# Two graph attention layers over 16 batches: layer 0's scores and V products in runs of two steps, tile additions in odd steps behind the minima, mask pieces later

## The chip, the cores and the metric

One core of one Trainium2 chip runs the whole program. The metric is device time in microseconds (us). Engines are named as in the profile: PE (TensorE, matmuls), PEld (its weight loads), DVE (VectorE), ACT (ScalarE), POOL (GpSimd), SP (SyncE, which issues most DMAs). SBUF is the on-chip memory of 128 partitions; PSUM is the memory that matmuls write.

## What is computed

The input x is 16 batches of 1024 rows by 256 features, adj is 16 matrices of 1024 by 1024 zeros and ones. Both layers are residual attention layers behind a layer norm and a ReLU:

```python
h = jnp.maximum(_layernorm(x), 0.0)
x = x + attention0(h, adj)        # 4 heads of 64, no biases but bo
h = jnp.maximum(_layernorm(x), 0.0)
x = x + attention1(h, adj)        # 8 heads of 32, bq, bk, bv, bo
# attention(h): q, k, v = h @ Wq, h @ Wk, h @ Wv, in heads
#   s = q k^T / sqrt(D);  s = where(adj > 0, s, -inf)
#   concat(softmax(s) v over heads) @ Wo + bo
```

All arithmetic is in float32; only the mask is held in 8 bits. Softmax is computed without subtracting a maximum; the sums are tested at the end (a slow program would run if a test failed; it did not run).

## The kernel before

**Steps.** The scores are held transposed, keys on the partitions. A *step* makes four blocks of 128 keys by 512 queries. Layer 0 has 16 steps per batch: two halves of the queries (`qh`), two groups of two heads (`g`), four steps `j` of two key tiles. Layer 1 has 32: `qh`, `g` (four heads), eight `j`. A step has these parts: `scores` (L364) makes four blocks in two PSUM pairs; `exponentials` takes for each pair VectorE's minimum with the mask (L380), which frees the pair, and ScalarE's exponential (L385); two steps later (`LEAD`) `weigh` (L396) multiplies by V into the group's PSUM tile `po`. PSUM score pairs come from one pool of three (`ps_s`), which K, Q, V, turns and output products (`pq`, `pv`, `ph`, `py`) use too.

**Row sums.** In layer 1 GpSimd adds the tiles of two steps (L482) and matmuls with ones count them (`count`, L273). In layer 0 `add_tiles` (L399 to L410) adds a step's two halves into a tile `t`: for `j` = 0 on GpSimd, for the others on VectorE (L407), and then GpSimd adds the tile of the step before (L409). The tiles come from a pool of three buffers. The last one of the group is counted once. Then `copy_out` (L280) copies the group's `po`, `spread` (L288 to L292) sends the sums through DRAM onto all partitions, `invert` (L297) takes reciprocals and sends them back by DRAM, `normalize` (L316) multiplies, `test` (L305 to L311) checks; `end_half` (L345, L350) makes the output product and adds it to x.

**Masks.** A mask comes in eight tiles: `load` (a DMA on POOL's queue, L121), `flip` (a transposing DMA on SP, L125), `put` (ScalarE, L131). The mask of layer 0 is then changed in place into that of layer 1 in eight pieces by VectorE (`second`, L139).

**Inputs of a section.** For each layer, batch and half: `stats` (VectorE, L160, L161), `norm` (ScalarE, L177), `add_bias` (GpSimd, L185), `turn` (transposes, L195), `k` and `q` (L207; copies L214, L220), `values` (L236).

**Order.** The order of everything is written out by hand; the engines run their queues in order of emission. All steps form one list: layer 0 of batch 0; then for each batch b layer 0 of b+1 and layer 1 of b. The table of due times (L597 to L641) says at which step each input, mask piece or load is emitted; `a` is the first step of layer 0 of b+1, and `c` that of layer 1 of b. `end_group` (L491 to L508) adds entries for the end of a group. `Stream.run` (L436 to L468) emits for each step i:

```python
if now: scores(now)
if i % 2 or not self.large(i):
    for st in waiting: weigh(st)          # else kept for the next step
    ...
exponentials(now, copy)                   # copy: between the two halves
add_tiles(step before), if layer 0
everything that is due at i
```

A *large* job (k, q, values, end_half) that is due at an even step puts off that step's weigh, so two steps' scores, then the large job, then two steps' scores and two weighs follow (a run of two). Where nothing large is due, scores and weigh alternate step by step.

**Start.** Before the stream (L511 to L567) come the loads of the first inputs, all eight flips and puts of mask 0, k, q and values of batch 0, and one product of `bv` with the output matrix (`pb`, L561), added to `bo` in `bo1` (L566).

Of the kernel before, what the change touches and what calls it, by code (L numbers as in the profile page):

```python
# [18 lines left out]
P = 128  # L19
EPS = 1e-5  # L20
HEADS = (4, 8)

LEAD = 2


SUM_MIN, SUM_MAX = 1e-15, 1e15
# [13 lines left out]
def load_weights(nc, const, a):  # L40

    w, loads = Weights(), []

    def mat(src, name):
        t = const.tile([P, 2, 256], F32, tag=name, name=name)
        loads.append((t, src.rearrange("(c p) f -> p c f", p=P)))
        return t

    def row(src, name):
        t = const.tile([P, 256], F32, tag=name, name=name)  # L50
        loads.append((t, src.partition_broadcast(P)))
        return t

    def col(src, name):
        t = const.tile([P, 2], F32, tag=name, name=name)
        loads.append((t, src.rearrange("(c p) -> p c", p=P)))
        return t

    w.k, w.q, w.v, w.o = [], [], [], []
    for layer in range(2):  # L60
        for kind, mats in (("k", w.k), ("q", w.q), ("v", w.v), ("o", w.o)):
            mats.append(mat(a[f"w{kind}{layer}"], f"w{kind}{layer}"))
    w.bo = [row(a["bo0"], "bo0"), row(a["bo1"], "bo1")]
    w.bq = col(a["bq1"], "bq1")
    w.bk = col(a["bk1"], "bk1")
    w.bv = col(a["bv1"], "bv1")
    w.ident = const.tile([P, P], F32, tag="ident", name="ident")
    make_identity(nc, w.ident)
    w.ones = const.tile([P, 64], F32, tag="ones", name="ones")
    nc.gpsimd.memset(w.ones, 1.0)  # L70
    w.mhalf = const.tile([P, 4], F32, tag="mhalf", name="mhalf")
    nc.gpsimd.memset(w.mhalf, -0.5)
    return w, loads


def fast_program(ctx, tc, a, w, loads, chk):
# [23 lines left out]

    def psum_pair(name):
        return ps_s.tile([P, 2, 512], F32, tag="ps_s", name=name)

    bo = [w.bo[0]]

    xs = {}

# [36 lines left out]
    class Inputs:  # L144
# [37 lines left out]
        def add_bias(self, half):  # L182

            rows = xs[self.b, half]
            nc.gpsimd.tensor_add(  # L185
                rows, rows, bo[self.layer].unsqueeze(1).to_broadcast([P, 4, E])
            )

        def turn(self, half):
# [56 lines left out]
    class Group:  # L246
# [21 lines left out]
        def count(self, p, start, stop):  # L268

            if start:  # L270
                self.s = ps_o.tile([P, 512], F32, tag="pz", name=f"pz_{self.n}")
            for r in range(self.per):
                nc.tensor.matmul(  # L273
                    self.s[r * self.D : (r + 1) * self.D, :], w.ones[:, : self.D], p[:, r, :],
                    start=start, stop=stop,
                )

        def copy_out(self):
            self.ob = work.tile([P, 512], F32, tag="o", name=f"o_{self.n}")
# [91 lines left out]
    def exponentials(st, between):  # L371
# [5 lines left out]
        for i in range(2):  # L377
# [6 lines left out]
            )  # L384
            nc.scalar.activation(half, half, AF.Exp, scale=gr.scale)  # L385
            if i == 0:
                between()

    def weigh(st):
        gr = st.gr  # L390
# [29 lines left out]
    class Stream:  # L420

        def __init__(self, steps):
            self.steps, self.due = steps, {}

        def large(self, i):
            return any(
                f.__name__ in ("k", "q", "values", "end_half") for f, _ in self.due.get(i, [])  # L430
            )

        def later(self, i, f, *args):
            self.due.setdefault(i, []).append((f, args))

        def run(self):  # L436
            steps = self.steps
# [2 lines left out]
            for i in range(n + LEAD):  # L440
# [2 lines left out]
                    waiting.append(steps[i - LEAD])  # L443
                if now:
                    scores(now)
                copy = lambda: None
                if i % 2 or not self.large(i):
                    for st in waiting:
                        weigh(st)
                    for st in waiting:  # L450
                        if st.gr.layer:
                            self.count_steps(i, st)
                        if st.last:
                            copy = st.gr.copy_out
                            self.end_group(i, st.gr)
                    waiting = []
                if now:
                    exponentials(now, copy)
                else:
                    copy()  # L460
                one = steps[i - 1] if 1 <= i <= n else None
                if one and one.gr.layer == 0:
                    add_tiles(one)
                for f, args in self.due.pop(i, []):
                    f(*args)
            while self.due:
                for f, args in self.due.pop(min(self.due)):
                    f(*args)  # L468
# [21 lines left out]

        def end_group(self, i, gr):  # L491

            if gr.layer == 0:
                i += 1
                self.later(i, gr.count, gr.t, True, True)
            elif not gr.hurry:
                i += 2
            self.later(i, gr.spread)
            if gr.hurry:
                self.later(i, gr.finish)  # L500
                self.later(i, gr.test)
                return
            self.later(i + 2, gr.invert)
            self.later(i + 3, gr.test)

            self.later(i + (5 if gr.layer and not gr.last else 4), gr.normalize)
            if gr.g == 1:
                self.later(i + (7 if gr.layer else 6), gr.end_half)  # L508

    def open_w(n):  # L510
        for _ in range(n):  # L511
# [13 lines left out]
    inp.stats(1)  # L525
    inp.turn(0)

    def tiles(*ts):
        for t in ts:
            mask.flip(t)  # L530
            (mask if t + 2 < NT else masks[1]).load((t + 2) % NT)
            open_w(-(-len(loads) // 2))

    tiles(0, 1)
    inp.k(0)
    inp.norm(1)
    inp.q(0)
    inp.turn(1)
    mask.put(0)
    mask.put(1)  # L540
    inp.values(0)
    tiles(2, 3)
    inp.k(1)
    mask.put(2)
    mask.put(3)
    tiles(4, 5)
    inp.q(1)
    mask.put(4)
    mask.put(5)
    tiles(6, 7)  # L550
    inp.values(1)
    mask.put(6)
    mask.put(7)
    for half in range(QH):
        open_x(1, half)
        inp.add_bias(half)


    pb = psum_pair("pb")[:, 0, :E]
    for c in range(2):  # L560
        nc.tensor.matmul(  # L561
            pb, w.bv[:, c : c + 1].to_broadcast([P, P]), w.o[1][:, c, :],
            start=(c == 0), stop=(c == 1),
        )
    bo1 = small.tile([P, E], F32, tag="bo1", bufs=1, name="bo1v")
    nc.vector.tensor_add(bo1, pb, w.bo[1])  # L566
    bo.append(bo1)  # L567

# [11 lines left out]
    stream = Stream(steps)  # L580
    later = stream.later

    def norms(inp, half, i):

        later(i, inp.stats, half, (0, 1))
        later(i + 1, inp.stats, half, (2, 3))
        later(i + 3, inp.norm, half, (0, 1))
        later(i + 4, inp.norm, half, (2, 3))
        later(i + 5, inp.add_bias, half)

    def half_inputs(inp, half, *at):

# [1 line left out]
            later(i, f, half)  # L594


    for t in range(NT):  # L597
        later(2 * t, masks[1].flip, t)
        later(2 * t + 1, masks[1].put, t)
        if t + 2 < NT:  # L600
            later(2 * t + 1, masks[1].load, t + 2)
    for half in range(QH):
        norms(inputs[0][1], half, 3 * half)
    half_inputs(inputs[0][1], 0, 5, 6, 8, 10)
    half_inputs(inputs[0][1], 1, 11, 12, 14, 16)
    for b in range(B - 1):
        mine, a, c = inputs[1][b], first[b + 1], second[b]
        if b == 0:

            norms(mine, 0, a + 1)  # L610
            norms(mine, 1, a + 9)
            half_inputs(mine, 0, a + 6, a + 8, a + 10, a + 12)
            half_inputs(mine, 1, a + 15, c, c + 4, c + 2)
        else:
            norms(mine, 0, a - 10)
            norms(mine, 1, a - 8)
            half_inputs(mine, 0, a - 4, a + 2, a + 4, a + 6)
            half_inputs(mine, 1, a - 2, a + 8, c + 4, c + 2)
        for kt in range(NT):
            later(a + 4 + kt, masks[b].second, kt)  # L620
        if b + 2 < B:
            other, mask = inputs[0][b + 2], masks[b + 2]
            later(a + 1, open_x, b + 2, 0)
            later(a + 11, open_x, b + 2, 1)
            norms(other, 0, a + 7)
            norms(other, 1, a + 15)
            half_inputs(other, 0, a + 14, c + 6, c + 10, c + 12)
            half_inputs(other, 1, c + 14, c + 16, c + 18, c + 20)
            for t in range(NT):
                i = a + 2 + 5 * t  # L630
                later(i, mask.load, t)
                later(i + 3, mask.flip, t)
                later(i + 5, mask.put, t)
        else:
            last = inputs[1][b + 1]
            norms(last, 0, c + 1)
            norms(last, 1, c + 9)
            half_inputs(last, 0, c + 6, c + 10, c + 12, c + 14)
            half_inputs(last, 1, c + 16, c + 20, c + 36, c + 34)
            for kt in range(NT):  # L640
                later(c + 8 + 2 * kt, masks[b + 1].second, kt)  # L641
    stream.run()
# [15 lines left out]

def careful_program(ctx, tc, a, w):

    nc = tc.nc
    x, adj, out = a["x"], a["adj"], a["out"]
    B, N, E = x.shape
    NT = N // P
    actp = ctx.enter_context(tc.tile_pool(name="cact", bufs=1))
    bv = actp.tile([P, E], F32, tag="bv", name="c_bv")
    nc.sync.dma_start(bv, a["bv1"].partition_broadcast(P))
# [6 lines left out]
    def layer_of(b, layer, xt):  # L674
# [26 lines left out]
        for t in range(NT):  # L701
            pv = ps_t.tile([P, E], F32, tag="t", name=f"c_pv_{layer}_{t}")
            for c in range(2):
                nc.tensor.matmul(
                    pv, hT[:, c, ts(t, P)], w.v[layer][:, c, :], start=(c == 0), stop=(c == 1)
                )
            if layer == 0:
                nc.scalar.copy(v[:, t, :], pv)
            else:
                nc.vector.tensor_add(v[:, t, :], pv, bv)  # L710
# [185 lines left out]
```

## Time and profile before

| what | us |
|---|---|
| median of 3 runs | 3406.17 (3405.55 to 3406.78) |
| the profiled execution | 3402.26 |
| its span | 3400.5 |
| busy: PE, DVE, POOL, ACT | 3359.3, 2468.8, 2446.0, 2188.1 |
| one period (layer 0 of one batch, layer 1 of the one before) | 209.40 |
| minimum L380, exponential L385, mean of one | 1.215, 1.057 |
| VectorE addition L407, median and mean | 1.219, 1.525 |
| GpSimd addition L409, mean; L482, mean | 2.495, 4.562 |
| mask piece L139, median and longest | 0.686, 4.417 |

The profile takes one execution. Its page lists for each engine the busy share, and for each line of the code the instructions: `p<-mask,ps 128x1024` reads as a tile p written from mask and ps, 128 partitions by 1024 elements, then the count, the busy time with the mean of one in ns, and the engine's idle time just before with what ended it (`<-PE ps L364` is a wait for the matmuls of that line). A timeline has start, duration, engine and line; it may join successive like instructions of one tile group in a row (x2, x8). A table by stretches has for each engine the busy time and, in brackets, the instructions; after them the granted clock of PE. Matmuls are float32, each with several passes, so that a block has more matmul rows than calls in the code.

### The profile page before, as it was taken

The numbers are of one execution on the slowest core, as the hardware profiler recorded it, in microseconds if no ns is written. First come the engines' busy times: TensorE is split into PE (matmuls) and PEld (weight loads), VectorE is DVE, ScalarE is ACT, GpSimd is POOL, SyncE is SP. The second block draws the span as 40 slices with busy tenths as digits, with TensorE's granted clock in tenths as the row PEclk, the third lists the DMA queues.
The fourth block names the chain that finished last, engine by engine and source line by source line (L and its number), as shares of the span: only waits on it lengthen the run. The fifth ranks groups of instructions, "written<-read, shape, count | busy, mean of one in ns | idle before, by whom it ended". The sixth has DMA issues, their size and how long they took to land. (4 is left out here: it accounts for less than half of the span.)

```text
span 3400.5 us, 46245 instructions
## 1 busy us (share of the span) xinstructions
PE 3359.3 (99%) x18190; PEld 1302.6 (38%) x18190; DVE 2468.8 (73%) x2664; ACT 2188.1 (64%) x2402; POOL 2446.0 (72%) x1606
## 2 busy tenths in 40 slices
PE   7999999999999999999999999999999999999998
PEld 3443343433434333343333334334343343433432
DVE  4676767777677776777767777677776777767876
ACT  5566666676666756667566675666756667565665
POOL 4577777777777776777668686686867768677777
PEclk9999999999999999999999999999999999999999
DMA  6212121211212122121111212112122111210001
GB/s 133 44 36 36 47 42 36 49 37 47 40 36 51 34 49 36 36 51 42 42 35 39 48 42 45 34 43 45 39 48 39 42 41 41 47 35 23 14 17 31
DMA packets 250737, 141.76 MB, mean 42 GB/s; under 512 B 182416, under 2 KB 217488, under 8 KB 250512
## 3 DMA queue, kind: packets, MB, share of 16 engines
q1 hardware_dynamic: 232080, 105.18, 12.6%
q0 software_dynamic: 18432, 33.56, 6.4%
q8 instruction: 144, 2.36, 0.3%
q14 instruction: 81, 0.66, 0.1%
HBM read 120.33 MB, written 18.34 MB: 41 GB/s over the span
## 5 line engine op out<-in xcount | busy, mean ns | idle before, releaser
L380 DVE SCALAR_TENSOR_TENSOR p<-mask,ps 128x1024 f32<-128x1024 fp8e4 x1536 | 1801.3, 1215 | 753.7 <-PE ps L364 729.1
L385 ACT ACTIVATE p<-p 128x1024 f32<-128x1024 f32 x1536 | 1618.2, 1057 | 984.1 <-DVE p L380 940.9
L482 POOL TENSOR_TENSOR p<-p,p 128x2048 f32<-128x2048 f32 x255 | 1163.0, 4562 | 399.9 <-PE po L396 396.1
L364 PE MATMUL ps<-qT,kT 32*128 32x512 f32 (+1 forms) x6144 | 1167.4, 633 | 13.1 <-DVE p L380 8.7
L396 PE MATMUL po<-p,v 128*32 128x512 f32 (+1 forms) x6144 | 989.9, 601 | 0.5 <-ACT o L280 0.5
L409 POOL TENSOR_TENSOR t<-t,t 128x1024 f32<-128x1024 f32 x192 | 479.1, 2495 | 401.3 <-DVE t L407 324.4
L364 PEld LDWEIGHTS ps<-qT,kT 32*128 32x128 f32 (+1 forms) x6144 | 375.0, 184 | 726.2 <-issue 364.0
L396 PEld LDWEIGHTS po<-p,v 128*32 128x32 f32 (+1 forms) x6144 | 229.1, 118 | 688.3 <-issue 529.3
L407 DVE TENSOR_TENSOR t<-p 128x1024 f32<-128x1024 f32 x192 | 292.7, 1525 | 0.9
L273 PE MATMUL pz<-p,ones 128*32 128x512 f32 x2056 | 267.8, 593 | 0.2 <-POOL p L482 0.2
L207 PE MATMUL pq<-hT,wk 128*128 128x512 f32 x512 | 240.0, 612 | 2.7 <-ACT hT L196 2.6
L236 PE MATMUL pv<-wv,hT 128*128 128x256 f32 x1024 | 237.9, 385 | 0.0
L345 PE MATMUL py<-wo,cat 128*128 128x256 f32 x1008 | 234.2, 385 | 2.5 <-DVE p L380 2.5
L207 PE MATMUL pq<-hT,wq 128*128 128x512 f32 x512 | 236.6, 605 | 0.0
L236 PEld LDWEIGHTS pv<-wv,hT 128*128 128x128 f32 x1024 | 189.4, 190 | 70.7 <-issue 36.1
L345 PEld LDWEIGHTS py<-wo,cat 128*128 128x128 f32 x1008 | 186.4, 190 | 73.2 <-issue 32.3
L316 POOL TENSOR_TENSOR cat<-o,inv 128x512 f32<-128x512 f32 x127 | 164.3, 1294 | 20.7 <-DMA inv<-vd 14.7
L407 POOL TENSOR_TENSOR t<-p 128x1024 f32<-128x1024 f32 x64 | 171.5, 2680 | 0.4
L131 ACT ACTIVATE mask<-adjT,mhalf 128x1024 fp8e4<-128x1024 bf16 x128 | 145.5, 1138 | 10.1 <-DMA adjT<-adj 10.1
L207 PEld LDWEIGHTS pq<-hT,wk 128*128 128x128 f32 x512 | 93.3, 192 | 144.3 <-issue 137.1
L207 PEld LDWEIGHTS pq<-hT,wq 128*128 128x128 f32 x512 | 92.1, 189 | 139.8 <-issue 128.5
L177 ACT ACTIVATE hn<-x,shift,rstd 128x256 f32<-128x256 f32 x256 | 138.1, 588 | 6.9 <-POOL shift L170 6.9
(52 smaller groups left out, 1567.8 us busy)
## 6 DMA issues: line engine op xcount, KB each, us to landing
adj<-in_adj_dram POOLq DMA_DIRECT2D x128, 256.0 KB, 3.6
x<-in_x_dram SPq DMA_DIRECT2D x32, 512.0 KB
inv<-vd SPq DMA_DIRECT2D x128, 128.0 KB
inv<-vd SPq DMA_DIRECT2D x252, 64.0 KB
out_dram<-x SPq DMA_DIRECT2D x31, 512.0 KB
adjT<-adj SPq DMA_TRANSPOSE x128
sd<-s SPq DMA_DIRECT2D x64, 4.0 KB
sn<-sd SPq DMA_DIRECT2D x64, 4.0 KB
```

The costliest lines, as they stand in the source:

```text
L207: nc.tensor.matmul(pq[:, m, :], wt[self.layer][:, c, ts(m, P)], self.hT[half][:, c, :], start=(c == 0), stop=(c == 1),)
L236: nc.tensor.matmul(pv[:, i, :], self.hT[half][:, c, ts(i, P)], w.v[self.layer][:, c, :], start=(c == 0), stop=(c == 1),)
L273: nc.tensor.matmul(self.s[r * self.D : (r + 1) * self.D, :], w.ones[:, : self.D], p[:, r, :], start=start, stop=stop,)
L316: nc.gpsimd.tensor_mul(self.half.cat[:, self.g, :], self.ob, self.inv)
L345: nc.tensor.matmul(py[:, i, :], self.half.cat[:, c, ts(i, P)], w.o[self.layer][:, c, :], start=(c == 0), stop=(c == 1),)
L364: nc.tensor.matmul(st.ps[i // 2][:, i % 2, :], gr.inp.kT[r * D : (r + 1) * D, gr.g, ts(kt, P)], gr.inp.qT[r * D : (r + 1) * D, gr.g, ts(gr ...
L380: nc.vector.scalar_tensor_tensor(out=half, in0=gr.mask.m[:, kt, ts(gr.qh, 512)].unsqueeze(1).to_broadcast([P, 2, 512]), scalar=BIG, in1=st ...
L385: nc.scalar.activation(half, half, AF.Exp, scale=gr.scale)
L396: nc.tensor.matmul(gr.o[r * D : (r + 1) * D, :], gr.inp.v[:, kt, h * D : (h + 1) * D], st.p[:, i, :], start=(kt == 0), stop=(kt == NT - 1),)
L407: engine.tensor_add(t, st.p[:, 0:2, :], st.p[:, 2:4, :])
L409: nc.gpsimd.tensor_add(t, t, gr.t)
L482: nc.gpsimd.tensor_add(one, one, st.p)
```

## The change

In `Stream.run`, a step of layer 0 with an even number never weighs: both steps' weighs come in the odd step. The tile additions of the two steps before are emitted in odd steps only, behind that step's minima. Counts are emitted ahead of the exponentials; layer 0's copy of `po` comes behind both. What is due at a step is sorted: small jobs first, turns and large jobs last. In `end_group` the delays change. In the start only masks 0's tiles 0 to 3 are flipped and put; tiles 4 to 7 and those of batch 1 follow at steps of the stream; the x of batch 1 is loaded earlier; layer 1's weights are loaded last; the product of `bv` moves to step 9. The due table is rewritten: layer 0's large jobs at odd steps, one k moved into layer 1's section, the pieces of `second` from a+5 on, two of them at a+7 and at a+11 each. The slow program's V bias is dropped; it does not run.

```diff
+LARGE = ("k", "q", "values", "end_half")
+COUNTS = ("count", "count_added")
...
+        def count_added(self):
+            self.count(self.t, True, True)
...
+        def rank(self, entry):
+            return entry[0].__name__ in ("turn", *LARGE)
...
-                copy = lambda: None
-                if i % 2 or not self.large(i):
+                copies = []
+                if i % 2 or not (now and now.gr.layer == 0 or self.large(i)):
                     for st in waiting:
                         weigh(st)
...
+                due = self.due.pop(i, [])
+                for f, args in due:
+                    if f.__name__ in COUNTS:
+                        f(*args)
                 if now:
-                    exponentials(now, copy)
+                    exponentials(now, copies if now.gr.layer else [])
+                    if now.gr.layer == 0:
+                        for f in copies:
+                            f()
...
-                one = steps[i - 1] if 1 <= i <= n else None
-                if one and one.gr.layer == 0:
-                    add_tiles(one)
-                for f, args in self.due.pop(i, []):
-                    f(*args)
+                if i % 2:
+                    for one in steps[max(i - 2, 0) : min(i, n)]:
+                        if one.gr.layer == 0:
+                            add_tiles(one)
+                for f, args in sorted(due, key=self.rank):
+                    if f.__name__ not in COUNTS:
+                        f(*args)
...
             if gr.layer == 0:
-                i += 1
-                self.later(i, gr.count, gr.t, True, True)
-            elif not gr.hurry:
-                i += 2
-            self.later(i, gr.spread)
...
-            self.later(i + 2, gr.invert)
-            self.later(i + 3, gr.test)
-            self.later(i + (5 if gr.layer and not gr.last else 4), gr.normalize)
+                self.later(i + 2, gr.count_added)
+                at = 2, 3, 4, 7
+            else:
+                at = (2, 3, 4, 8) if gr.last else (2, 4, 7, 9)
+            for k, f in zip(at, (gr.spread, gr.invert, gr.normalize)):
+                self.later(i + k, f)
+            self.later(i + at[1] + 1, gr.test)
             if gr.g == 1:
-                self.later(i + (7 if gr.layer else 6), gr.end_half)
+                self.later(i + at[3], gr.end_half)
...
-    mask.put(6)
-    mask.put(7)
...
+    def flip(u):
+        masks[u // NT].flip(u % NT)
+        if u + 2 < 2 * NT:
+            masks[(u + 2) // NT].load((u + 2) % NT)
+    def put(u):
+        masks[u // NT].put(u % NT)
...
+    flip(2)
+    open_x(1, 0)
+    flip(3)
+    open_w(5)
+    open_x(1, 1)
...
+    for u in range(4, 2 * NT):
+        later(u - 3, flip, u)
+        later(u - 2, put, u)
+    later(9, bias_of_v)
...
-            norms(mine, 0, a - 10)
-            norms(mine, 1, a - 8)
-            half_inputs(mine, 0, a - 4, a + 2, a + 4, a + 6)
-            half_inputs(mine, 1, a - 2, a + 8, c + 4, c + 2)
+            norms(mine, 0, a - 10, a - 9, a - 7, a - 6)
+            half_inputs(mine, 0, a + 1, a + 3, a + 5, a + 7)
+            norms(mine, 1, a - 8, a - 7, a - 5, a - 4)
+            half_inputs(mine, 1, a + 11, c + 2, c + 6, c + 4)
         for kt in range(NT):
-            later(a + 4 + kt, masks[b].second, kt)
+            later(a + 5 + (0, 2, 2, 4, 6, 6, 8, 10)[kt], masks[b].second, kt)
...
-            norms(other, 0, a + 7)
-            norms(other, 1, a + 15)
-            half_inputs(other, 0, a + 14, c + 6, c + 10, c + 12)
-            half_inputs(other, 1, c + 14, c + 16, c + 18, c + 20)
+            norms(other, 0, a + 5, a + 7, a + 9, a + 11)
+            half_inputs(other, 0, a + 13, c + 10, c + 12, c + 14)
+            norms(other, 1, c + 5, c + 7, c + 9, c + 10)
+            half_inputs(other, 1, c + 15, c + 18, c + 20, c + 24)
```

The new function `bias_of_v` holds the product that stood in the start, and writes `bo` in place instead of a tile of its own. `norms` and `half_inputs` take their steps one by one (turn, k, q, values); the entries of the first two and the last batches are shifted likewise.

More of the change, by code (lines that the diff above doesn't have):

```diff
@@ L59, in load_weights, with mats @@
     w.k, w.q, w.v, w.o = [], [], [], []
-    for layer in range(2):
-        for kind, mats in (("k", w.k), ("q", w.q), ("v", w.v), ("o", w.o)):
-            mats.append(mat(a[f"w{kind}{layer}"], f"w{kind}{layer}"))
+    def mats(layer):
+        for kind, of in (("k", w.k), ("q", w.q), ("v", w.v), ("o", w.o)):
+            of.append(mat(a[f"w{kind}{layer}"], f"w{kind}{layer}"))
+    mats(0)
     w.bo = [row(a["bo0"], "bo0"), row(a["bo1"], "bo1")]
@@ L66, in load_weights @@
     w.bv = col(a["bv1"], "bv1")
+    mats(1)
     w.ident = const.tile([P, P], F32, tag="ident", name="ident")
@@ L102, in psum_pair @@
         return ps_s.tile([P, 2, 512], F32, tag="ps_s", name=name)
-    bo = [w.bo[0]]
     xs = {}
@@ L185, in add_bias @@
             nc.gpsimd.tensor_add(
-                rows, rows, bo[self.layer].unsqueeze(1).to_broadcast([P, 4, E])
+                rows, rows, w.bo[self.layer].unsqueeze(1).to_broadcast([P, 4, E])
             )
@@ L386, in exponentials @@
             if i == 0:
-                between()
+                for f in between:
+                    f()
     def weigh(st):
@@ L429, in large @@
             return any(
-                f.__name__ in ("k", "q", "values", "end_half") for f, _ in self.due.get(i, [])
+                f.__name__ in LARGE for f, _ in self.due.get(i, [])
             )
@@ L453, in run @@
                         if st.last:
-                            copy = st.gr.copy_out
+                            copies.append(st.gr.copy_out)
                             self.end_group(i, st.gr)
                     waiting = []
+                due = self.due.pop(i, [])
+                for f, args in due:
+                    if f.__name__ in COUNTS:
+                        f(*args)
                 if now:
-                    exponentials(now, copy)
-                else:
-                    copy()
-                one = steps[i - 1] if 1 <= i <= n else None
-                if one and one.gr.layer == 0:
-                    add_tiles(one)
-                for f, args in self.due.pop(i, []):
-                    f(*args)
+                    exponentials(now, copies if now.gr.layer else [])
+                    if now.gr.layer == 0:
+                        for f in copies:
+                            f()
+                else:
+                    for f in copies:
+                        f()
+                if i % 2:
[5 more added lines that the diff above has]
+                        f(*args)
             while self.due:
@@ L491, in end_group @@
         def end_group(self, i, gr):
+            if gr.hurry:
+                for f in (gr.spread, gr.finish, gr.test):
+                    self.later(i, f)
+                return
             if gr.layer == 0:
-                i += 1
-                self.later(i, gr.count, gr.t, True, True)
-            elif not gr.hurry:
-                i += 2
-            self.later(i, gr.spread)
[L499 to L502, printed above, removed]
-            self.later(i + 2, gr.invert)
-            self.later(i + 3, gr.test)
-            self.later(i + (5 if gr.layer and not gr.last else 4), gr.normalize)
+                self.later(i + 2, gr.count_added)
[5 more added lines that the diff above has]
+            self.later(i + at[1] + 1, gr.test)
             if gr.g == 1:
-                self.later(i + (7 if gr.layer else 6), gr.end_half)
+                self.later(i + at[3], gr.end_half)
     def open_w(n):
@@ L526, in fast_program @@
     inp.turn(0)
[L528 to L534, printed above, removed]
+    def flip(u):
[4 more added lines that the diff above has]
+        masks[u // NT].put(u % NT)
+    flip(0)
+    flip(1)
+    open_w(1)
     inp.k(0)
@@ L538, in fast_program, with bias_of_v @@
     inp.turn(1)
-    mask.put(0)
-    mask.put(1)
+    put(0)
+    put(1)
     inp.values(0)
-    tiles(2, 3)
+    flip(2)
[3 more added lines that the diff above has]
+    open_x(1, 1)
     inp.k(1)
-    mask.put(2)
-    mask.put(3)
-    tiles(4, 5)
+    put(2)
+    put(3)
     inp.q(1)
-    mask.put(4)
-    mask.put(5)
-    tiles(6, 7)
     inp.values(1)
-    mask.put(6)
-    mask.put(7)
+    open_w(len(loads))
     for half in range(QH):
-        open_x(1, half)
         inp.add_bias(half)
[L559 to L567, printed above, removed]
+    def bias_of_v():
+        pb = psum_pair("pb")[:, 0, :E]
+        for c in range(2):
+            nc.tensor.matmul(
+                pb, w.bv[:, c : c + 1].to_broadcast([P, P]), w.o[1][:, c, :],
+                start=(c == 0), stop=(c == 1),
+            )
+        nc.vector.tensor_add(w.bo[1], pb, w.bo[1])
     steps = layer_steps(inputs[0][0], masks[0])
@@ L581, in fast_program, with norms @@
     later = stream.later
[L583 to L589, printed above, removed]
+    def norms(inp, half, *at):
+        for i, f in zip(at, (inp.stats, inp.stats, inp.norm, inp.norm)):
+            later(i, f, half, (0, 1) if i in (at[0], at[2]) else (2, 3))
+        later(at[3] + 1, inp.add_bias, half)
     def half_inputs(inp, half, *at):
@@ L594, in half_inputs @@
             later(i, f, half)
[L597 to L605, printed above, removed]
+    for u in range(4, 2 * NT):
+        later(u - 3, flip, u)
+        later(u - 2, put, u)
+    later(9, bias_of_v)
+    norms(inputs[0][1], 0, 1, 2, 4, 5)
+    half_inputs(inputs[0][1], 0, 7, 9, 9, 11)
+    norms(inputs[0][1], 1, 5, 6, 8, 9)
+    half_inputs(inputs[0][1], 1, 11, 13, 15, 15)
     for b in range(B - 1):
@@ L608, in fast_program @@
         if b == 0:
[L610 to L613, printed above, removed]
-        else:
-            norms(mine, 0, a - 10)
-            norms(mine, 1, a - 8)
-            half_inputs(mine, 0, a - 4, a + 2, a + 4, a + 6)
-            half_inputs(mine, 1, a - 2, a + 8, c + 4, c + 2)
+            norms(mine, 0, a + 1, a + 2, a + 4, a + 5)
+            half_inputs(mine, 0, a + 7, a + 9, a + 11, a + 13)
+            norms(mine, 1, a + 9, a + 10, a + 12, a + 13)
+            half_inputs(mine, 1, a + 15, c + 2, c + 6, c + 4)
+        else:
+            norms(mine, 0, a - 10, a - 9, a - 7, a - 6)
+            half_inputs(mine, 0, a + 1, a + 3, a + 5, a + 7)
+            norms(mine, 1, a - 8, a - 7, a - 5, a - 4)
+            half_inputs(mine, 1, a + 11, c + 2, c + 6, c + 4)
         for kt in range(NT):
-            later(a + 4 + kt, masks[b].second, kt)
+            later(a + 5 + (0, 2, 2, 4, 6, 6, 8, 10)[kt], masks[b].second, kt)
         if b + 2 < B:
@@ L623, in fast_program @@
             later(a + 1, open_x, b + 2, 0)
-            later(a + 11, open_x, b + 2, 1)
-            norms(other, 0, a + 7)
-            norms(other, 1, a + 15)
-            half_inputs(other, 0, a + 14, c + 6, c + 10, c + 12)
-            half_inputs(other, 1, c + 14, c + 16, c + 18, c + 20)
+            later(a + 10, open_x, b + 2, 1)
+            norms(other, 0, a + 5, a + 7, a + 9, a + 11)
+            half_inputs(other, 0, a + 13, c + 10, c + 12, c + 14)
+            norms(other, 1, c + 5, c + 7, c + 9, c + 10)
+            half_inputs(other, 1, c + 15, c + 18, c + 20, c + 24)
             for t in range(NT):
@@ L634, in fast_program @@
         else:
[L635 to L639, printed above, removed]
+            last, e = inputs[1][b + 1], c + 32
+            norms(last, 0, c + 1, c + 2, c + 4, c + 5)
+            half_inputs(last, 0, c + 9, c + 12, c + 14, c + 16)
+            norms(last, 1, c + 9, c + 10, c + 12, c + 13)
+            half_inputs(last, 1, c + 17, c + 20, e + 6, e + 4)
             for kt in range(NT):
@@ L665, in careful_program @@
     actp = ctx.enter_context(tc.tile_pool(name="cact", bufs=1))
-    bv = actp.tile([P, E], F32, tag="bv", name="c_bv")
-    nc.sync.dma_start(bv, a["bv1"].partition_broadcast(P))
     work = ctx.enter_context(tc.tile_pool(name="cwork", bufs=2))
@@ L706, in layer_of @@
                 )
[L707 to L710, printed above, removed]
+            nc.scalar.copy(v[:, t, :], pv)
         for half in range(N // 512):
```

## The prediction

> **What bounds the kernel now.** I read the shares of busy time first, then the stretches of one batch, then the waits, then the timelines of TensorE and VectorE in one batch.
>
> ```profile
> PE 3359.3 (99%) x18190; PEld 1302.6 (38%) x18190; DVE 2468.8 (73%) x2664; ACT 2188.1 (64%) x2402; POOL 2446.0 (72%) x1606
> ...
> 1401.31:1483.47 82.16, 82.16 (x352) 30.66 (x348) 62.18 (x66) 46.98 (x54) 59.57 (x42) 1.00 0.18 42
> 1483.47:1610.71 127.24, 127.10 (x790) 50.43 (x788) 91.34 (x102) 89.61 (x98) 93.81 (x60) 1.00 0.20 41
> ```
>
> TensorE (PE) is busy 99% of the span, at a granted clock of 0.996. The two stretches are layer 0 of batch 7 and layer 1 of batch 6, one period of 209.40 us; layer 0 alone has no idle TensorE. VectorE (DVE) and GpSimd (POOL) work 62.2 and 59.6 us of layer 0's 82.2. So the kernel can gain only by cheaper successions of matmuls or by taking out TensorE's waits, and it loses when VectorE falls behind: TensorE writes scores to PSUM, VectorE's minima free it, and there are three pairs for the two that a step takes. The fourth pair allocated waits for the first half's minimum of the step before.
>
> I priced TensorE's blocks by the time from first matmul to next first matmul, in the undisturbed places of the timeline: a layer-0 score half 0.96; a layer-0 weigh 1.77 behind a score block, 1.82 behind another weigh; 1.87 alone between two scores (1466.30 to 1470.09, 3.79 us, is S S W); K or Q 3.63, V 3.65, Y 3.65, T 1.02, C 0.96 to 1.01. By these prices 3287 of TensorE's 3381 us from first to last block are matmuls and 94 are waits: 12.4 in layer 0 of batch 0, 0.03 in each later layer 0, 4.8 in each later layer 1 (8.7 and 4.9 in the last two).
>
> **Part 1, the order on TensorE.** The instruction order of the changed kernel holds the same 3610 matmul rows of blocks. In layer 0, five steps of a period that stood alone (S S W) become pairs (S S S S W W): 3.58 instead of 3.73 for two weighs, and C and T stand with them; one K moves to layer 1 and two T come from it. Summed block by block: layer 0 from 82.1 to 79.8 per period, layer 1 without waits from 122.4 to 123.8; -0.9 per period, -11 in 13. The first two and the last sections, whose order differs more, give -9 by the same sum. Together **-20 us**.
>
> **Part 2, layer 1's waits.** Of the 4.8, 2.5 lie in three lone steps in a row (c+22 to c+26, c its first step); four more of 0.5 to 0.7 behind a T or a lone weigh. In the new order the large blocks cover all but four separate pairs; with the second score half late by 0.4 to 1.0 as in those places, 2.7 remain: -2.1 x 13 = **-27**.
>
> **Part 3, VectorE in layer 0.** A step's two minima are 1.22 each and start 1.14 apart. Now the tile additions of two steps come together in an odd step, and mask pieces behind them. This decides the case. The rows:
>
> ```profile
> L380 DVE SCALAR_TENSOR_TENSOR p<-mask,ps 128x1024 f32<-128x1024 fp8e4 x1536 | 1801.3, 1215 | 753.7 <-PE ps L364 729.1
> ...
> L409 POOL TENSOR_TENSOR t<-t,t 128x1024 f32<-128x1024 f32 x192 | 479.1, 2495 | 401.3 <-DVE t L407 324.4
> ...
> L407 DVE TENSOR_TENSOR t<-p 128x1024 f32<-128x1024 f32 x192 | 292.7, 1525 | 0.9
> ```
>
> An undisturbed addition is 1.22 (the median), yet the mean is 1.53: VectorE's additions are held up by GpSimd's. Two timelines of before show how. First, the usual case:
>
> ```profile
> 1441.12 1.22 DVE L407 TENSOR_TENSOR t<-p 128x1024 f32<-128x1024 f32 x1
> ...
> 1442.25 0.69 DVE L139 TENSOR_SCALAR mask<-mask 128x1024 fp8e4<-128x1024 fp8e4 x1
> 1442.41 2.74 POOL L409 TENSOR_TENSOR t<-t,t 128x1024 f32<-128x1024 f32 x1 [2.52 <-DVE t L407]
> ```
>
> The mask piece, queued right behind the addition, starts before GpSimd's addition; GpSimd's then takes 2.74 instead of 2.37, as if held until the piece has ended at 1442.94. Second, what happens where GpSimd already waits:
>
> ```profile
> 173.92 2.35 POOL L185 TENSOR_TENSOR x<-x,bo1v 128x1024 f32<-128x1024 f32 x1
> 173.99 3.37 DVE L407 TENSOR_TENSOR t<-p 128x1024 f32<-128x1024 f32 x1
> ...
> 176.24 2.25 POOL L316 TENSOR_TENSOR cat<-o,inv 128x512 f32<-128x512 f32 x1
> 177.28 1.75 DVE L139 TENSOR_SCALAR mask<-mask 128x1024 fp8e4<-128x1024 fp8e4 x1
> ```
>
> The addition is held to the end of GpSimd's bias addition (176.27), GpSimd's next instruction (1.28 alone) takes 2.25, as if held until the addition's end at 177.36, and the mask piece behind it takes 1.75, ending 0.54 after GpSimd's. So the one that waited got its turn first. It is one instance; I take it as the rule.
>
> A layer 0 has eight pairs of steps, counted from 0, two per group. In the changed order the second pair of each group (1, 3, 5, 7) has in VectorE's queue: four minima, addition of tile j1, addition of j2, mask pieces (two in pairs 3 and 5, one in 7). In pairs 3, 5 and 7 the waits of the order show that the addition of j2 waits for GpSimd's addition of j1: the pool of three t tiles gives j2 the buffer of j0, which that addition reads. Before, the same wait stood a step later and was long met. Now:
> - addition j1, 1.22; GpSimd's j1 2.37 + 0.08; addition j2 1.22; first piece 0.69; GpSimd's j2, waiting, goes next (2.2 left to run after the piece); the second piece ends 0.55 behind it. With the minima 4.54: 12.9. Pair 3 has 1.2 of statistics too, 13.9 with the overlap of starts.
> - TensorE's blocks in pair 3 take 12.0, in pair 5 9.4. VectorE is late by 1.9 and 3.5; the PSUM rotation forgives about 0.5 at the second. What is queued behind the waiting piece is the next step's minima, and the scores wait for those.
> - So the next pairs' scores wait 1.9 and 3.1: 5.0 per section against 0.03. In pair 7 (10.1 against 8.4, with one piece) I put 0.6 at layer 1's second step, which is in part 2.
> 5.0 x 13 = **+65**. The bounds are 0 (VectorE catches up in the type of pair without the wait, 7.9 of 10.9) and 7.5 (both waits in full, and nothing forgiven).
>
> The Trainium skill, "SBUF — State Buffer", section "Who interferes with whom", states that a VectorE instruction with two SBUF inputs and a GpSimd one that reads SBUF exclude each other for the whole instruction, and that whoever starts first holds the port. This speaks against putting pieces behind additions, and the rows above agree (3.37 instead of 1.22). It does not say who comes next when one has waited. The page "TensorEngine Tiling (Array Packing)", "Key Properties", says that a switch of array mode drains the array, which speaks for runs of two; the rows price a saved switch at only 0.15 per two weighs.
>
> **Part 4, start and edges.** In the start, ScalarE's mask conversions (1.13 each, 10.1 us idle before them for the transposes) of pieces 4 to 7 go behind the first steps, the exponentials no longer queue behind them, and the weights of layer 1 load later. Of the 12.4 us of waits in batch 0's layer 0 I let 4.5 stand: **-8**; bounds 0 and -12. The new DMA queue order on SP puts two x loads between the transposes; that is in the bound. Batch 1's layer 0 gets mask pieces and conversions together, +6, and the layer 0 of batch 15 the 5 of part 3; the others (layer 1 of batch 0 -1.5, of 14 -0.8, of 15 +0.5) sum to -2: **+9**. The counts ahead of the exponentials, the copies of sums behind both exponentials and the later delays of spread, invert and normalize move ScalarE and GpSimd work with 30% free; cost 0, hidden by TensorE. If that cover goes, a reciprocal that waits for its 7 us round trip through DRAM would hold VectorE's queue up, 0.5 to 2 us per group.
>
> **Sum.** -20 - 27 + 65 - 8 + 9 = +19 on the profiled execution's 3402.3: 3421. The median of the runs shown is 3.9 above it, so **3425 us**.
>
> **Rivals.**
> 1. *The second piece is not held.* If VectorE goes on with the next queued piece and GpSimd waits on, pair 3 is 11.7 against 12.0 and pair 5 10.7 against 9.4: 0.9 per section instead of 5.0, 13 x 4.1 = 53 less, 8 less at the edges and at layer 1's entry: **3364**, faster. For it: the usual case above, where the queued piece went first. Against it: 176.24. It decides from a layer-0 wait under 3.5 us per section (19/13 below 5.0), which is break-even.
> 2. *VectorE is never late*, because the tile wait also fits (GpSimd's addition overlaps the statistics, or the pool gives another buffer): layer 0 stays at 0, **3347**. For it: 20 us free per section. Against: the waits in the order.
> 3. *More is late.* 71 of 192 additions were held before; if the additions of j1 find GpSimd busy for another 1 us in pairs 3 and 5, that is 2 x 15 more, **3455**. For it: GpSimd's normalize (1.28) and bias (2.37) stand in those pairs too.
> 4. *The change does not do what it says* (pairs not formed): excluded by the instruction order, under 0.01.
>
> **How the numbers follow.** Forecast 0.50, rival 1 0.22, rival 2 0.12, rival 3 0.15. The forecast's own range is 3408 to 3440 (start 0 to -12, layer-0 wait 4 to 6). The range goes from 3352 to 3446: it leaves out most of rival 2 and two thirds of rival 3. A measurement of this kernel can tell about 0.2%, 7 us. Faster: rivals 1 and 2 and a trace of the forecast, 0.36; same (3399 to 3413): the forecast's lower end, 0.10; slower 0.54.
>
> **What would show it.** In the profile after: waits of the scores for VectorE's minima, or the late minima themselves, in pairs 4 and 6 of each layer 0, of 2 and 3 us; layer 0 of batch 7 at 84.8 us (79.8 + 5.0) and layer 1 of batch 6 at 126.5; the mean of a mask piece up from 0.80 to about 1.3, with every second piece near 2.8 in pairs 3 and 5; the addition of j2 starting 2.45 behind the end of j1's. If layer 0 takes 80 to 81, rival 1 or 2 holds, told apart by the pieces' durations. The number would be wrong also if the start gives nothing or if layer 1 keeps its 4.8.

## The result, and the profile after

The change made the kernel slower: 3493.3 us (median; 3492.1 to 3494.9) against 3405.9, a ratio of 1.0258 (95% interval 1.0241 to 1.0276), 87 us. The forecast was 3425, its range 3352 to 3446: the sign was right, the size a quarter. The profiled execution took 3494.0, with a span of 3492.2 against 3400.5. From the page after (same columns as before):

```profile
PE 3343.9 (96%) x18190; PEld 1312.9 (38%) x18190; DVE 2459.0 (70%) x2664; ACT 2192.1 (63%) x2402; POOL 2426.2 (69%) x1606
...
L388 DVE SCALAR_TENSOR_TENSOR p<-mask,ps 128x1024 f32<-128x1024 fp8e4 x1536 | 1791.4, 1213 | 639.5 <-PE ps L372 571.0
...
L372 PE MATMUL ps<-qT,kT 32*128 32x512 f32 (+1 forms) x6144 | 1133.8, 634 | 100.4 <-DVE p L388 85.5
...
L418 POOL TENSOR_TENSOR t<-t,t 128x1024 f32<-128x1024 f32 x192 | 494.8, 2577 | 517.8 <-DVE t L416 511.1
...
L416 DVE TENSOR_TENSOR t<-p 128x1024 f32<-128x1024 f32 x192 | 233.0, 1220 | 129.4 <-POOL t L418 129.4
L278 PE MATMUL pz<-p,ones 128*32 128x512 f32 x2056 | 268.5, 594 | 24.3 <-POOL p L509 22.9
...
L144 DVE TENSOR_SCALAR mask<-mask 128x1024 fp8e4<-128x1024 fp8e4 x128 | 159.0, 1262 | 0.0
```

TensorE has about 15 us less busy time and much more idle time, and the last column says on whom: its scores wait 85.5 us for VectorE's minima (8.7 before) and its counts 22.9 for GpSimd's pair sums (0.2 before). VectorE's additions are no longer held (mean 1.22, 1.53 before), but VectorE stands idle for 129 us ahead of them, waiting for GpSimd's additions (0.9 before); the mean of a mask piece rose from 0.80 to 1.26. Of the engines' busy times, only ScalarE's (by 4 us) and the weight loads' (by 10) are up.

The table by stretches of the kernel after, for layer 0 of batch 8 and layer 1 of batch 7 (columns as shown before):

```profile
1649.40:1737.69 88.29, 80.77 (x361) 32.01 (x357) 62.90 (x65) 48.77 (x53) 59.38 (x45) 0.98 0.20 45
1737.69:1864.30 126.61, 126.49 (x782) 49.58 (x780) 89.90 (x102) 88.15 (x97) 92.31 (x57) 1.00 0.17 36
```

A layer 0 takes 88.3 instead of 82.2, with 7.5 of TensorE idle, and its mean clock is 0.98. Layer 1 is 0.6 shorter. Means over the sections (first score matmul to that of the next section): layer 0 of batches 2 to 14 82.16 before, **88.71** after (84.8 forecast); layer 1 of batches 1 to 13 127.25 before, **126.99** after (126.5 forecast). 13 x 6.55 is 85 of the 91 us that the blocks lost.

**Pair 5 and pair 6.** The timeline of the kernel after, all engines, in that layer 0:

```profile
1698.88 1.13 PE L372 MATMUL ps<-qT,kT 64*128 64x512 f32 x4 [1.76 <-DVE p L388]
...
1712.95 1.22 DVE L416 TENSOR_TENSOR t<-p 128x1024 f32<-128x1024 f32 x1
...
1714.24 2.36 POOL L418 TENSOR_TENSOR t<-t,t 128x1024 f32<-128x1024 f32 x1 [3.20 <-DVE t L416]
...
1716.64 1.23 DVE L416 TENSOR_TENSOR t<-p 128x1024 f32<-128x1024 f32 x1 [2.48 <-POOL t L418]
...
1717.78 3.44 DVE L144 TENSOR_SCALAR mask<-mask 128x1024 fp8e4<-128x1024 fp8e4 x2
1717.94 2.72 POOL L418 TENSOR_TENSOR t<-t,t 128x1024 f32<-128x1024 f32 x1 [1.34 <-DVE t L416]
...
1721.14 2.34 DVE L388 SCALAR_TENSOR_TENSOR p<-mask,ps 128x1024 f32<-128x1024 fp8e4 x2
...
1722.40 2.08 PE L372 MATMUL ps<-qT,kT 64*128 64x512 f32 x4 [3.28 <-DVE p L388]
```

These rows show the queue as forecast: addition j1, 2.48 of idle for GpSimd's j1, addition j2, then two pieces that take 3.44 where two undisturbed ones in a row take 1.29 (`even_pieces`, at 1651.52), since the second is held until GpSimd's j2 ends at 1720.66. The minimum that frees the scores' PSUM starts at 1721.14, and TensorE has been idle for 3.28. (Waits of pairs 4 and 6 are given below by the block prices of the prediction, 1.82 and 3.34 here, 0.06 above the idle in the rows.) What was not forecast is the duration in the last line: these four matmuls take 2.08, where the four of the first line take 1.13. The clock has gone down, as the table of stretches shows (the granted clock is the 0.50):

```profile
1722.23:1725.64 3.41, 3.24 (x8) 1.04 (x10) 3.41 (x5) 3.19 (x4) 1.78 (x2) 0.50 0.30 43
```

**The entry.** The same timeline, at the first pair of the section (it begins at 1649.40):

```profile
1648.28 2.42 POOL L190 TENSOR_TENSOR x<-x,bo 128x1024 f32<-128x1024 f32 x1
...
1651.99 4.54 POOL L509 TENSOR_TENSOR p<-p,p 128x2048 f32<-128x2048 f32 x1
...
1656.56 2.35 DVE L388 SCALAR_TENSOR_TENSOR p<-mask,ps 128x1024 f32<-128x1024 fp8e4 x2 [3.57 <-POOL p L509]
1656.58 1.07 PE L278 MATMUL pz<-p,ones 128*32 128x512 f32 x8 [1.63 <-POOL p L509]
...
1660.38 1.01 ACT L201 COPY hT<-ph 128x1024 f32<-128x1024 f32 x1
...
1661.44 1.99 PE L372 MATMUL ps<-qT,kT 64*128 64x512 f32 x8 [0.85 <-ACT hT L201]
```

GpSimd's last but one pair sum of the section before starts 2.6 behind the section's start. In the kernel before it was 0.5, in the rows of the section that starts at 1610.71:

```profile
1610.71 1.99 PE L364 MATMUL ps<-qT,kT 64*128 64x512 f32 x8
...
1611.25 4.55 POOL L482 TENSOR_TENSOR p<-p,p 128x2048 f32<-128x2048 f32 x1
```

In the kernel after, two wait for it: TensorE's count, and VectorE's minimum, which wants its `p` buffer. The minimum makes ScalarE late, and ScalarE's copy of the turn, which frees a PSUM pair, holds the next scores for another 0.85. Together 2.7 by the block prices (2.48 of idle).

### The profile page after: what moved, and what is told of

Read it like the earlier page. It is cut to its first block, busy times and chain, and to the rows that moved or that the text cites. A ratio compares the mean times of both kernels' runs of the same rounds, so it can differ in the third digit from the quotient of the medians.

```text
span 3492.2 us, 46291 instructions
## 1 busy us (share of the span) xinstructions
PE 3343.9 (96%) x18190; PEld 1312.9 (38%) x18190; DVE 2459.0 (70%) x2664; ACT 2192.1 (63%) x2402; POOL 2426.2 (69%) x1606
## 5 line engine op out<-in xcount | busy, mean ns | idle before, releaser
L372 PE MATMUL ps<-qT,kT 32*128 32x512 f32 (+1 forms) x6144 | 1133.8, 634 | 100.4 <-DVE p L388 85.5
L418 POOL TENSOR_TENSOR t<-t,t 128x1024 f32<-128x1024 f32 x192 | 494.8, 2577 | 517.8 <-DVE t L416 511.1
L405 PEld LDWEIGHTS po<-p,v 128*32 128x32 f32 (+1 forms) x6144 | 240.0, 120 | 700.9 <-issue 551.4
L416 DVE TENSOR_TENSOR t<-p 128x1024 f32<-128x1024 f32 x192 | 233.0, 1220 | 129.4 <-POOL t L418 129.4
L278 PE MATMUL pz<-p,ones 128*32 128x512 f32 x2056 | 268.5, 594 | 24.3 <-POOL p L509 22.9
L190 POOL TENSOR_TENSOR x<-x,bo 128x1024 f32<-128x1024 f32 x64 | 159.7, 2496 | 1.6 <-DMA bo<-in_bo_dram 1.5
L144 DVE TENSOR_SCALAR mask<-mask 128x1024 fp8e4<-128x1024 fp8e4 x128 | 159.0, 1262 | 0.0
L416 POOL TENSOR_TENSOR t<-p 128x1024 f32<-128x1024 f32 x64 | 151.0, 2360 | 2.2 <-ACT p L393 2.2
```

Of the source, the lines that this page charges most:

```text
L278: nc.tensor.matmul(self.s[r * self.D : (r + 1) * self.D, :], w.ones[:, : self.D], p[:, r, :], start=start, stop=stop,)
L372: nc.tensor.matmul(st.ps[i // 2][:, i % 2, :], gr.inp.kT[r * D : (r + 1) * D, gr.g, ts(kt, P)], gr.inp.qT[r * D : (r + 1) * D, gr.g, ts(gr ...
L405: nc.tensor.matmul(gr.o[r * D : (r + 1) * D, :], gr.inp.v[:, kt, h * D : (h + 1) * D], st.p[:, i, :], start=(kt == 0), stop=(kt == NT - 1),)
L416: engine.tensor_add(t, st.p[:, 0:2, :], st.p[:, 2:4, :])
L418: nc.gpsimd.tensor_add(t, t, gr.t)
```

## Experiments

All numbers beside the medians are means over the same sections as above.

| kernel | median us | ratio to before (95%) | layer 0 | layer 1 |
|---|---|---|---|---|
| before | 3405.9 | | 82.16 | 127.25 |
| after | 3493.3 | 1.0241 to 1.0276 | 88.71 | 126.99 |
| t4 | 3441.0 | 1.0091 to 1.0125 | 86.69 | 126.39 |
| one_piece | 3433.2 | 1.0075 to 1.0113 | 84.22 | 127.31 |
| adds_each_step | 3408.6 | 1.0003 to 1.0022 | 82.52 | 127.99 |
| t4_even_pieces | 3379.8 | 0.9911 to 0.9944 | 81.16 | 127.46 |
| even_pieces | 3442.1 | 1.0096 to 1.0130 | 82.57 | 129.19 |
| bias_later | 3451.5 | 1.0120 to 1.0154 | 85.83 | 126.72 |
| t4_even_bias | 3335.6 | 0.9779 to 0.9812 | 78.20 | 127.11 |
| small2 | 3493.8 | 1.0243 to 1.0277 | 88.60 | 126.94 |
| before_mends | 3414.8 | 1.0016 to 1.0036 | 82.16 | 128.11 |
| mended2 | 3318.8 | 0.9727 to 0.9760 | 78.20 | 125.99 |

**t4: a fourth t buffer.**

```diff
-    small = ctx.enter_context(tc.tile_pool(name="small", bufs=4))
+    small = ctx.enter_context(tc.tile_pool(name="small", bufs=2))
...
-        t = work.tile([P, 2, 512], F32, tag="t", bufs=3, name=f"t_{st.n}")
+        t = work.tile([P, 2, 512], F32, tag="t", bufs=4, name=f"t_{st.n}")
```

> The changed kernel with four t buffers instead of three (the pool of small tiles goes from four to two buffers for the room), so the addition of j2 no longer waits for GpSimd's addition of j1. Theory A (two causes in VectorE's queue, the buffer wait and the turn that a waiting GpSimd addition gets ahead of the next queued VectorE instruction): the wait comes back at the mask pieces. Addition j1, addition j2 at once, then GpSimd's j1 goes ahead of the first piece (2.4), GpSimd's j2 ahead of the second (2.4): the sum stays 12.9 in pair 5, layer 0 of batch 8 stays at 88.3 +- 1 us, the median at 3485 to 3495. Rival R1 (the buffer wait alone, the pieces are harmless): layer 0 at 82 to 83, the median near 3410. Rival R2 (four score halves in a row ask for more PSUM pairs than there are, whatever VectorE's order): 3493 unchanged.

The timeline of pair 3 of batch 8:

```profile
1658.14 2.35 DVE L416 TENSOR_TENSOR t<-p 128x1024 f32<-128x1024 f32 x2
...
1659.44 6.03 POOL L418 TENSOR_TENSOR t<-t,t 128x1024 f32<-128x1024 f32 x2 [3.34 <-DVE t L416]
...
1660.41 5.60 DVE L144 TENSOR_SCALAR mask<-mask 128x1024 fp8e4<-128x1024 fp8e4 x2
```

The two additions now follow each other at once, and the time comes back in the pieces: 5.60 instead of 3.44, each held behind one of GpSimd's additions. The waits of pairs 4 and 6 fall only from 1.82 and 3.34 to 1.43 and 2.94. That is theory A, and R1 falls. Yet the median moved by 52, not by at most 8. Part of it is the start: layer 0 of batch 0 went from 91.2 to 84.0 and of batch 1 from 98.4 to 90.6. In batch 0 there are no pieces, so there the fourth buffer takes the whole wait away (TensorE's idle of 4.79 at 71 us is gone). Another part, in the start too, is the clock: the stretches at half clock fall from 86 to 37 us in the whole run, which at half speed is some 24 of the 52. Two sections of this one run show what such a stretch costs:

```profile
1405.02:1492.64 87.62, 80.92 (x360) 32.02 (x356) 68.18 (x67) 48.77 (x53) 61.14 (x45) 0.98 0.19 45
1619.17:1705.11 85.94, 79.22 (x361) 31.62 (x357) 68.18 (x67) 48.65 (x53) 61.70 (x44) 1.00 0.20 46
1478.60:1482.00 3.40, 3.40 (x10) 0.98 (x8) 3.40 (x4) 3.40 (x4) 0.31 (x2) 0.50 0.60 119
1691.50:1694.90 3.40, 3.40 (x16) 1.08 (x18) 3.40 (x5) 3.33 (x4) 1.48 (x2) 1.00 0.40 54
```

These are layer 0 of batches 7 and 8, and the 3.4 us that follow TensorE's longest idle in each. Both sections have the same waits, the longest 2.87; in batch 7 a stretch at a granted clock of 0.50 follows it, in batch 8 none, and batch 7 is 1.68 longer.

**small2: the control for that room.** Only the pool of small tiles is cut to two, with three t buffers.

> A control: the changed kernel with two instead of four buffers of small tiles and nothing else, as the four t buffers needed the room. Expected 3493 within 5; if it moves by more, the time of the run with four t buffers has to be read against it.

3493.8, as expected; the smaller pool costs nothing.

**one_piece: one mask piece in each odd step.**

```diff
-            later(a + 5 + (0, 2, 2, 4, 6, 6, 8, 10)[kt], masks[b].second, kt)
+            later(a + 1 + 2 * kt, masks[b].second, kt)
```

> The changed kernel with one mask piece in each odd step (a+1, a+3 to a+15) instead of two in pairs 3 and 5; the buffer wait stays. Theory A: the second piece's 2.75 leaves VectorE's queue; pair 5 is 10.1 against TensorE's 9.4, pair 3 within its 12.0; the waits of 1.8 and 3.3 fall to 0 and 0.2, the half-clock stretch of 1.65 that follows the longer of them goes too; what remains is the 2.7 at the entry of layer 0: layer 0 of batch 8 at 81.5 to 82.5, median 3400 to 3412. R1: the buffer wait of 2.45 is left and costs as much, layer 0 over 86, median over 3460. R2: 3493 unchanged.

Pair 4 no longer waits, pair 6 waits 0.6: so far A, and R2 falls. But the median missed by over 20. The first piece, at a+1, meets a pair sum of the layer before:

```profile
1622.20 4.55 POOL L509 TENSOR_TENSOR p<-p,p 128x2048 f32<-128x2048 f32 x1
...
1623.31 3.98 DVE L144 TENSOR_SCALAR mask<-mask 128x1024 fp8e4<-128x1024 fp8e4 x1
```

It takes 3.98, ends 0.54 behind that sum, and puts 1.4 of idle into pair 1. With the entry's 1.6 and 0.85, that is three short idles within 10 us, and in 6 of 14 sections the clock was halved after the third. The expectation had looked at GpSimd's additions of layer 0 only.

**adds_each_step: one addition behind each step's minima.**

```diff
-                if i % 2:
-                    for one in steps[max(i - 2, 0) : min(i, n)]:
+                if i:
+                    for one in steps[i - 1 : min(i, n)]:
```

> The changed kernel with one tile addition behind each step's minima, even ones too, as before the change; mask pieces stay where the change put them. Theory A: the addition of j1 stands a step ahead of that of j2, GpSimd has 2.27 of minima to finish; the second piece is still held. Pair 3 11.6 against 12.0, pair 5 10.6 against 9.4: the waits fall to 0 and 0.7, no half clock: layer 0 of batch 8 near 82.5, median 3405 to 3420. R1: the same layer 0 less 0.7, median near 3400. R2: 3493 unchanged.

As A expected: pair 6 waits 1.1, layer 0 is 82.5, and no stretch of half clock comes before layer 1 of batch 14. Undoing this one part of the change takes back 85 of the 87 us. It does not make a gain: the entry's 2.7 and pair 6's 1.1 eat what the order on TensorE saves in layer 0, and layer 1 is 0.7 longer than before.

**even_pieces and t4_even_pieces: pieces in even steps, where no addition is queued.**

```diff
-            later(a + 5 + (0, 2, 2, 4, 6, 6, 8, 10)[kt], masks[b].second, kt)
+            later(a + (2, 2, 6, 6, 10, 10, 14, 14)[kt], masks[b].second, kt)
```

> The changed kernel with three t buffers as it has, the mask pieces two at a time in even steps (a+2, a+6, a+10, a+14). It leaves the buffer wait alone in VectorE's queue. Theory A: pair 5 has minima 4.54, pieces 1.38, addition j1 1.22, the wait 2.45, addition j2 1.22 = 10.8 against 9.4: 0.9 of wait in pair 6 (1.4 less the 0.5 that the rotation forgives), none in pair 4, no half clock; layer 0 of batch 8 at 82 to 82.5, median 3390 to 3402. A theory in which the buffer wait costs what it lasts puts 2.4 in each of pairs 4 and 6, layer 0 at 86, median over 3440.

> Four t buffers, and the mask pieces two at a time in even steps (a+2, a+6, a+10, a+14), behind two minima and ahead of the next two, where no addition is queued and GpSimd should have ended its own. Theory A: both causes are gone; VectorE 8.4 in pair 5; layer 0 of batch 8 at 81 to 82 (the entry's 2.7 stays), median 3395 to 3408. R1: the same. R2: 3493 unchanged.

With both, layer 0 has only the entry left (81.16), and the median, 3379.8, was lower than expected: the start's waits, which the expectation left out, went too. With the pieces alone layer 0 was as A has it (82.57, pair 6 waits 1.2). The median was missed by 40, mostly because the lateness of pair 7, which now has two pieces beside the buffer wait, shows behind the section's end: layer 1 is 2.2 longer than after, 1.5 of it behind its first output product. In batch 0 (90.9) the buffer wait is as it was.

**bias_later: GpSimd's bias additions out of the end of layer 1.**

```diff
-        later(at[3] + 1, inp.add_bias, half)
+        later(bias or at[3] + 1, inp.add_bias, half)
...
-            norms(mine, 0, a - 10, a - 9, a - 7, a - 6)
+            norms(mine, 0, a - 10, a - 9, a - 7, a - 6, bias=c + 3)
...
-            norms(mine, 1, a - 8, a - 7, a - 5, a - 4)
+            norms(mine, 1, a - 8, a - 7, a - 5, a - 4, bias=c + 7)
```

> The changed kernel with GpSimd's two bias additions for layer 1's inputs moved from the last steps of the section before (a-5 +- and a-3) to c+3 and c+7 of their own layer 1 (batches 1 on). Theory E (the entry): the two additions of 2.42 put GpSimd's last pair sums back; TensorE's count waits 1.8 for them and, behind it, a score half 0.9 for ScalarE's copy. Without them the 2.7 at the entry of each layer 0 go: layer 0 of batch 8 at 85.5 to 86 (pairs 4 and 6 and the half clock stay), median 3493 - 14 x 2.7 = 3455 +- 6. Rival: the pair sums, 4.56 each, are too slow by themselves for the last four steps, or the late count is due to its place ahead of the exponentials; then 3485 to 3495.

Layer 0 fell by 2.9 to 85.83, the median to 3451.5: both waits of the entry are gone, the others stand. So the entry is a cause of its own.

**t4_even_bias and mended2: all three.** mended2 has four t buffers, the bias additions later, and the pieces at `a + (2, 2, 4, 6, 6, 8, 10, 10)[kt]`.

> Four t buffers, pieces in even steps, and the bias additions later, together. If the three causes are separate, the sections of layer 0 stand at 78.5 to 79.5 (the sum of their blocks) and the median at 3380 - 14 x 2.7 = 3342, between 3338 and 3352; if GpSimd's queue only moves its delay to layer 1, 3365 to 3380.

> The changed kernel with four t buffers and the later bias additions, the pieces in even steps a+2 (two), a+4, a+6 (two), a+8, a+10 (two), none in the last two pairs. In the mended run before, layer 1's first two steps wait 1.2 behind pair 7, where VectorE has two pieces; without them about 0.7 x 14 = 9 less: 3322 to 3330. If the single pieces at a+4 and a+8 meet GpSimd's additions there (up to 2.4 each), the sections of layer 0 stay at 78 only as far as the next pair's 11 us allow; then 3335 to 3345.

t4_even_bias took 3335.6, a little under its range, with layer 0 at 78.20: the three causes are separate. The stretches of layer 0 of batch 8 and layer 1 of batch 7 in mended2:

```profile
1562.08:1640.28 78.20, 78.20 (x360) 32.00 (x356) 61.35 (x66) 47.63 (x53) 56.61 (x37) 1.00 0.21 51
1640.28:1766.30 126.02, 126.02 (x784) 49.50 (x783) 89.97 (x102) 88.94 (x98) 98.24 (x65) 1.00 0.18 38
```

Layer 0 is 78.20 in each of the 13 sections, with TensorE busy to the last tenth; TensorE's scores wait 5.8 us for minima in the whole run. mended2 takes 3318.8, 2.6% less than before (0.9727 to 0.9760), a little under the 3322 to 3330 expected: without pieces in pair 7 layer 1 is 1.1 shorter than in t4_even_bias, where 0.7 was expected. It beats both kernels, and every part of the change's order on TensorE is still in it.

**before_mends: the same mends in the kernel before** (even pieces and later biases; three t buffers).

> A control: the kernel before the change with the same mends, as far as there is room: pieces two at a time in even steps, bias additions of layer 1's inputs at c+3 and c+7 (three t buffers as before). If the gain of the mended changed kernel comes from the change (fewer switches and waits on TensorE) once its three new waits are gone, the mends do nothing here, since before had 0.03 of waits in a layer 0: 3400 to 3410. If they are a gain by themselves, 3380 or less.

It is 0.3% slower than before, a little above the 3400 to 3410 expected: layer 0 as it was (82.16), layer 1 0.9 longer. These two mends are worth nothing without the change. The fourth t buffer and the places that mended2 gives the pieces were not tried in the kernel before; but VectorE's additions had only 0.9 us of idle ahead of them there in the whole run, and its layer 0 had no TensorE idle to win back. So the gain is the change's order on TensorE.

## Why the prediction was wrong

- **The order on TensorE (part 1)** was right in its direction, and the saving was put too small: layer 0 without waits 79.8 forecast, 78.2 measured (mended2), from 82.2.
- **Layer 1's waits (part 2)**: -2.1 x 13 forecast. Layer 1's mean fell by 0.26, where part 1 had it 1.4 longer and part 2 2.1 shorter, -0.7: about 6 us too hopeful.
- **VectorE in layer 0 (part 3)**: the mechanism and both waits were right (1.9 and 3.1 forecast, 1.82 and 3.34 measured, 0.03 before), and the one instance at 174 us did show the rule. Rivals 1 and 2 are out: the pieces were held in every section. Rival 3 came nearest by its number (3455), but its cause did not occur: no addition was held (mean 1.22). The first step that failed is the price of these waits, 5.0 x 13 = +65, which counts each wait at its own length and the clock behind it at nothing. TensorE's idle of 3.27 to 3.28 was followed by a half-clock stretch in all 14 sections, of 3.41 or 6.83 us; that costs 1.7 or 3.4 more per section. In the whole run the half-clock stretches grew from 27 to 86 us, which at half speed is about 29 of the 87. The profile before had shown it: of the four idles of 2.45 to 6.12 between its first and last scores, three were followed by half clock (those of 2.46, 6.12 and 2.55).
- **"Cost 0" with "30% free" (part 4)** is the second step that failed, for GpSimd. A mean share says nothing of the last eight steps of layer 1. There the change itself took away the waits and turns that had given GpSimd time: from the output product's step to layer 0's start TensorE needs 19.5 instead of 22.0 (1629.86 to 1649.40; 1588.68 to 1610.71), while GpSimd has the same pair sums, two bias additions and tests. Two turns of TensorE's (1.02 each) are gone from that stretch; from the second of GpSimd's pair sums in it to the late one its queue takes 15.1 in both kernels (1636.89 to 1651.99; 1596.20 to 1611.25). The entry's wait for GpSimd cost 2.7 x 14 = 38. No rival named it.
- **The start (part 4)**: -8 for batch 0 was about right in the order itself (94.4 before, 84.0 in the run with four t buffers), but after the change the buffer wait there let TensorE idle for 4.79 and a half-clock stretch of 6.83 followed (91.2). Layer 0 of batches 0 and 1 together took 3 more than before, where the forecast had -8 and +6 beside their share of part 1's -9.

The sum: 13 sections of layer 0 at 3.9 over the forecast are 51 of the 73 missed (2.7 entry, 2.0 clock, less 0.8 elsewhere); layer 1 6; the first two and the last sections 17 (9 longer than before, -9 - 8 + 9 = -8 forecast). What stays open is why the pool gives j2 the buffer of j0 and not a free one; the order shows the wait, and one more buffer ends it.

## What to carry to other kernels

Two instructions of one engine that are emitted together can be late by what other engines put between them: write down what each waits for, and which waiting instruction of the neighbour gets its turn ahead of the next. A wait of the bounding engine has to be priced with the clock that follows it. And when a stretch of the bounding engine gets shorter, look at the engine that had been keeping pace in just that stretch, not at its mean share.

## What the runs showed of the hardware

- **The clock.** Of TensorE's idles of 3.27 to 3.28 us in layer 0 after, 14 of 14 were followed by the granted clock of 0.50; of those of 2.87 to 2.88 in t4, 6 of 14; of those of 1.6 to 1.8 after, 1 of 27. With small2 (14 of 14) and bias_later (13 of 14) it is 41 of 42 for 3.26 to 3.29. The stretches in layer 0 after last 3.41 or 6.83. The Trainium skill, "TensorE: Matmul & The Clock Gate", "HAM oscillation — how this bites in real kernels", warns of idle gaps over some 3.4 us; here shorter ones were enough, as the same page's free-running window of that length (in Part 1) would allow, when the little that TensorE did beside the gap is counted as idle. That last is an inference, and the one case behind an idle of 1.77 strains it; the counts decide.
- **Who comes next.** Where a VectorE and a GpSimd instruction hold each other up, the one that was waiting when the other ended went next in all the rows read, so two additions and two pieces alternate with GpSimd's two additions (t4). A held piece ended 0.54 to 0.56 behind the GpSimd instruction that held it, whatever its length (3.98 behind a pair sum, 2.75 behind an addition).
